# Results used later in three places of a four-layer network: leaky relu, pooled rows, a block's first channel sums

## The chip, the cores and the metric

The kernel runs on one core of a Trainium2 chip, in float32 throughout. The metric is the device time of one execution in microseconds (us); the time of a kernel is the median over its runs.

A core has five engines that each work off a list of instructions in order and wait for each other by semaphores: TensorE (PE, matmuls and transposes into PSUM; its weight loads are listed as PEld), VectorE (DVE), ScalarE (ACT), GpSimd (POOL) and SyncE (SP, which here issues the plain DMAs).[...]

## The reference

Four layers of 256 channels act on four images of 64 x 64 pixels; each normalises its input over groups of eight channels (`_gn`) and adds its result to it. Layer 0 is a deformable convolution with a feed-forward part, layer 1 a linear attention, layer 2 a 3 x 3 convolution with binarised weights, layer 3 a softmax attention in which keys and values come from the image pooled 2 x 2. Of these, the change touches the sampling and the feed-forward part of layer 0 and the pooling of layer 3:

```
        samp = _grid_sample(img, sg)
        mr = mask.reshape(n, H * W, G, P).transpose(0, 2, 1, 3).reshape(n * G, 1, H * W, P)
        dout = (samp * mr).sum(-1).reshape(n, G * GC, H * W).transpose(0, 2, 1).reshape(n, H, W, C)
        dout = jnp.einsum('nhwc,oc->nhwo', dout, outproj_w) + outproj_b
        x2 = _bn(inp + dout, bn2_g, bn2_b, bn2_m, bn2_v, 3)
...
        hmid = jax.nn.leaky_relu(jnp.einsum('nhwc,oc->nhwo', x3, fc1_w) + fc1_b, SLOPE)
        m = jnp.einsum('nhwc,oc->nhwo', hmid, fc2_w) + fc2_b
        return (inp + m).transpose(0, 3, 1, 2)
...
        theta = _conv1x1(x, theta_w, theta_b)
        xp = _maxpool2x2(x)
        phi = _conv1x1(xp, phi_w, phi_b)
        gi = _conv1x1(xp, g_w, g_b)
```

## The kernel before

Channels lie on the 128 partitions (two tiles of them, `KT` = 2); an image of 4096 pixels is worked on in eight blocks of 512 (`NB`). Each step is a Python generator that issues some instructions and yields a cost. `beside` (in `run`) steps one main generator and hands each of the others its share of the way by those costs. Under `ordered()` the order in which instructions are issued on PE, DVE, ACT and POOL is kept as written; SP's is not in that list.

The stages, in order: layer 0's first convolution for image 0; then `sample` for the images 0 to 3, each with other work beside it (convolutions of the other images beside image 0; from image 1 on, the feed-forward part of the image before in the first fifth, then its layer 1, and from image 2 on layers 2 and 3 of the image before that); then, without any gather left, the last image's feed-forward part, layer 1 and what remains of layers 2 and 3.

`sample` goes in rounds of 14 pixels, 293 per image; up to 16 rounds make a block of up to 224 pixels, 19 per image. In each round POOL issues four indirect DMAs (L592), which gather 128 rows each into a tile `g` (seven buffers). PE multiplies them with the weights `wm` (made by DVE, L583, four rounds at a time) and sums them into one half of the PSUM tile `acc` (L599). Two rounds make a unit, which fills that half. A unit that ends in round i is then passed on by work kept in `later`, at the head of the rounds that follow, ahead of their gathers:

- in round i + 1, `moved`: ACT copies the half to `at` (L604)
- in round i + 2, `turned`: PE transposes `at` into one half of the PSUM tile `dp` (L609)
- in round i + 3, `spread`: ACT copies that into the block's `dT`, twice (L624); `dT` has one buffer

After a block's last round i, `project` (PE, L632), `add` (DVE, L636) and `finish` (ACT, L641, with its sum read out, and a store by SP, L644) follow for the first channel tile in rounds i + 4, i + 5 and i + 6 and for the second one round later each. So `spread` of the next block's first unit stands in the same round as the second `project`, behind it. Entries of one round run in the order in which they were entered.

`feedforward` loads its weights, works out a gate per channel, folds it into `f1`, and goes through the eight blocks: for each of eight tiles of hidden channels a matmul into a PSUM bank (L717), then `leaky`: ACT writes slope times the value into `lk` (L173; two buffers), DVE takes the larger of that and the value into `hm` (L174). Then for each of two tiles 16 matmul instructions over `hm` (L724) and DVE's addition to the residual `xyf` (L725), DVE's statistics of the result (L110) and its store (L728). Each matmul of 512 columns is two instructions in the profile. The banks come from a rotation of three (`ps`), which the projections `po` and other work share.

`layer3` first goes through its eight blocks: load `x5` (L154), the theta matmul (L1074), ACT's copy with bias (L1075), DVE's two maxima for the pooling (`m1`, L1079, then `xq`, L1082), and then on `xq` the phi and g matmuls (L1087, L1089) and their copies (L1090 ACT, L1091 DVE). The attention over all pixels follows.

Of the kernel before, what the change touches and what calls it, by code (L numbers as in the profile page):

```python
# [9 lines left out]
F32 = mybir.dt.float32  # L10
I32 = mybir.dt.int32
AF = mybir.ActivationFunctionType
ALU = mybir.AluOpType
# [4 lines left out]
P = 128  # L18
N, C, H, W = 4, 256, 64, 64
HW = H * W  # L20
KT = C // P
NB = HW // 512
# [7 lines left out]
RP, WR, UR, BR = 14, 4, 2, 16  # L30
# [5 lines left out]
SLOPE = 0.01  # L36
# [35 lines left out]
class Net:  # L72
# [92 lines left out]
    def row(self, name):  # L165
        at, n = ROWS[name]
        return self.rows[:, at:at + n]

    def leaky(self, pool, out, ps, bias, low):

        nc = self.nc
        t = pool.tile([P, 512], F32, name="lk")
        nc.scalar.activation(t, ps, AF.Identity, bias=low, scale=SLOPE)  # L173
        nc.vector.scalar_tensor_tensor(out, ps, bias, t, ALU.add, ALU.max)  # L174

    def depthwise(self, acc, src, w, k, rows, cols, r0, bias=None, step=lambda cost: cost, out=None):

# [370 lines left out]
    def sample(self, n, ssum):  # L548
# [4 lines left out]
        nc, sp = self.nc, self.sp  # L553
# [34 lines left out]
        def gathered(sl, wm, acc, r):  # L588
            r4, acc = r % WR, acc[:, r % UR * P:(r % UR + 1) * P]
            g = self.gp.tile([P, G, 256], F32, name="g", bufs=7)  # L590
            for i in range(G):
                nc.gpsimd.indirect_dma_start(  # L592
                    out=g[:, i, :], out_offset=None, in_=table,
                    in_offset=bass.IndirectOffsetOnAxis(ap=sl.bitcast(I32)[:, r, i:i + 1], axis=0))


            for x in range(2):
                for i in range(G):
                    nc.tensor.matmul(acc[32 * i:32 * i + 32, :], wm[:, r4, 4 * i + 2 * x:4 * i + 2 * x + 2, :],  # L599
                                     g[:, i, x * P:(x + 1) * P], start=x == 0, stop=x == 1)  # L600
# [48 lines left out]
        for i, (b, r) in enumerate(order):  # L649
            for f in later.pop(i, ()):  # L650
                f()
            sl, rounds = blocks[b]
            if r % UR == 0:
                acc = next(accs)
            gathered(sl, wm, acc, r)
            if r == 0 and b + 1 < len(BLOCKS):
                load(b + 1)
            ends = r + 1 == len(rounds)
            if r % WR == 0:
                if r + WR < len(rounds):  # L660
                    nxt = weigh(b, r + WR)
                elif b + 1 < len(BLOCKS):
                    nxt = weigh(b + 1, 0)
            if r % UR == UR - 1 or ends:
                unit = rounds[r - r % UR:r + 1]
                todo = [partial(moved, acc, len(unit), i), partial(turned, len(unit), i), partial(spread, unit, b, i)]
                todo = list(enumerate(todo, i + 1))
                if ends:
                    todo += [(i + 4 + m + j, partial(f, b, m)) for m in range(KT) for j, f in enumerate((project, add, finish))]
                for j, f in todo:  # L670
                    later.setdefault(j, []).append(f)
            if r % WR == WR - 1 or ends:
                wm = nxt
            yield 1
# [5 lines left out]
    def feedforward(self, n, ssum, st):  # L680
        nc, tc, a = self.nc, self.tc, self.a
        with tc.tile_pool(name=f"fa{n}", bufs=1, side="right") as sp, \
                tc.tile_pool(name=f"fb{n}", bufs=2, side="right") as bp:
            f1 = sp.tile([P, KT, 4 * C], F32, name="f1")
            nc.sync.dma_start(f1, a["fc1_wT"])
            f2 = sp.tile([P, 4 * KT, C], F32, name="f2")
            nc.sync.dma_start(f2, a["fc2_wT"])
            sd = sp.tile([P, KT, 64], F32, name="sd")
            nc.sync.dma_start(sd, a["se_down_wT"])
            su = sp.tile([64, C], F32, name="su")  # L690
            nc.sync.dma_start(su, a["se_up_wT"])
            mean = sp.tile([P, KT], F32, name="mean")
            nc.vector.tensor_reduce(mean, ssum, AX.X, ALU.add)
            nc.vector.tensor_scalar(mean, mean, 1.0 / HW, None, ALU.mult)
            ps = self.ps()
            for k in range(KT):
                nc.tensor.matmul(ps[0:64, 0:1], sd[:, k], mean[:, k:k + 1], start=k == 0, stop=k == KT - 1)
            dn = sp.tile([64, 1], F32, name="dn")
            nc.scalar.activation(dn, ps[0:64, 0:1], AF.Relu, bias=self.vec("se_down_b")[0:64])
            yield 2  # L700
            ex = sp.tile([P, KT], F32, name="ex")
            for m in range(KT):
                ps = self.ps()
                nc.tensor.matmul(ps[:, 0:1], su[:, m * P:(m + 1) * P], dn, start=True, stop=True)
                nc.scalar.activation(ex[:, m:m + 1], ps[:, 0:1], AF.Sigmoid, bias=self.vec("se_up_b", m))

            for k in range(KT):
                nc.scalar.activation(f1[:, k], f1[:, k], AF.Identity, scale=ex[:, k:k + 1])  # L708
            yield 6
            for b in range(NB):  # L710
                x2 = self.block(bp, self.x2_d[n], b, "x2f")
                xy = self.block(bp, self.xy_d[n], b, "xyf")
                hm = bp.tile([P, 4 * KT, 512], F32, name="hm", bufs=1)
                for m in range(4 * KT):
                    ps = self.ps()
                    for k in range(KT):
                        nc.tensor.matmul(ps, f1[:, k, m * P:(m + 1) * P], x2[:, k], start=k == 0, stop=k == KT - 1)  # L717
                    self.leaky(bp, hm[:, m], ps, self.vec("fc1_b", m), self.low1[:, m:m + 1])
                    if m % 2:
                        yield 5  # L720
                for m in range(KT):
                    ps = self.ps()
                    for k in range(4 * KT):
                        nc.tensor.matmul(ps, f2[:, k, m * P:(m + 1) * P], hm[:, k], start=k == 0, stop=k == 4 * KT - 1)  # L724
                    nc.vector.tensor_tensor(xy[:, m], xy[:, m], ps, ALU.add)  # L725
                    yield 10
                self.stats(st, xy, b)
                nc.sync.dma_start(self.x3_d[n][:, :, b * 512:(b + 1) * 512], xy)  # L728


    def layer1(self, n, st, st2):
# [301 lines left out]
    def layer3(self, n, st, wide=False):  # L1033
        nc, tc, a = self.nc, self.tc, self.a
        M = HW // 4
        with tc.tile_pool(name=f"na{n}", bufs=1, side="left") as sp, \
# [17 lines left out]
            ps = self.ps()  # L1054
# [12 lines left out]
            th = sp.tile([P, HW], F32, name="th")  # L1067
            ph = sp.tile([P, M], F32, name="ph")
            gt = sp.tile([P, 8, P], F32, name="gt")
            for b in range(NB):  # L1070
                x = self.block(bp, self.x5_d[n], b, "x5", tag="pT")
                ps = self.ps()
                for k in range(KT):
                    nc.tensor.matmul(ps, tw[:, k], x[:, k], start=k == 0, stop=k == KT - 1)  # L1074
                nc.scalar.activation(th[:, b * 512:(b + 1) * 512], ps, AF.Identity, bias=tb)  # L1075

                m1 = bp.tile([P, KT, 256], F32, name="m1", tag="pe")
                v = x.rearrange("p k (x d) -> p k x d", d=2)
                nc.vector.tensor_tensor(m1, v[:, :, :, 0], v[:, :, :, 1], ALU.max)  # L1079
                v = m1.rearrange("p k (r d x) -> p k r d x", d=2, x=W // 2)  # L1080
                xq = bp.tile([P, KT, P], F32, name="xq", tag="m2")
                nc.vector.tensor_tensor(xq.rearrange("p k (r x) -> p k r x", x=W // 2),  # L1082
                                        v[:, :, :, 0], v[:, :, :, 1], ALU.max)
                yield 4
                ps = self.ps()
                for k in range(KT):
                    nc.tensor.matmul(ps[:, 0:P], fw[:, k], xq[:, k], start=k == 0, stop=k == KT - 1)  # L1087
                for k in range(KT):
                    nc.tensor.matmul(ps[:, P:2 * P], xq[:, k], gw[:, k], start=k == 0, stop=k == KT - 1)  # L1089
                nc.scalar.activation(ph[:, b * P:(b + 1) * P], ps[:, 0:P], AF.Identity, bias=fb)  # L1090
                nc.vector.tensor_tensor(gt[:, b], ps[:, P:2 * P], gb, ALU.add)  # L1091
                yield 2


            tv = th.rearrange("p (n j) -> p j n", j=NT)
            for b in range(NB):
                m2 = bp.tile([P, 512], F32, name="m2")
                for j in range(4):
# [27 lines left out]
                    ps = self.ps()  # L1126
# [4 lines left out]
                r = self.block(bp, self.x5_d[n], b, "r5", bufs=1)  # L1131
                for k in range(KT):
                    ps = self.ps()
# [169 lines left out]
```

## Time and profile before

| what | value |
|---|---|
| runs | 7858.98 us median (7857.48 to 7888.82, three runs) |
| profiled execution | 8957.1 us, mean granted TensorE clock 0.804 |
| image 0's gathers | 190 to 1983 us |
| image 1's gathers | 1983 to 3751 us |
| image 2's gathers | 3751 to 5589 us |
| image 3's gathers | 5592 to 7430 us |
| feed-forward parts | 2046 to 2389, 3809 to 4155, 5646 to 5994, 7480 to 7703 us |
| layer 3's pooling loops | 4620 to 4730, 6464 to 6572, 8011 to 8095, 8762 to 8787 us |

The profile is of one execution, which took longer than the runs without a profiler. A line of the groups reads: source line, engine, operation, output from inputs, shapes, count, then busy time and mean duration, then how long the engine stood idle just before these instructions and what ended most of that idle time. A releaser named "remote" or "issue" is one that the profile doesn't resolve. Ends of matmuls are modelled.

### The profile page before, as it was taken

How to read it: one execution, taken by the hardware profiler on the slowest of the kernel's cores; microseconds unless marked ns; L12 is line 12 of the kernel's file. 1: busy time of each engine (PE TensorE's matmuls, PEld its weight loads, DVE VectorE, ACT ScalarE, POOL GpSimd, SP SyncE). 2: the span in 40 equal slices, each digit the busy share in tenths (PEclk: the TensorE clock that was granted, in tenths of full speed). 3: DMA queues.
4: the chain of work that ended last, by engine and by line, in shares of the span. 5: the costliest groups of instructions: out<-in, count | busy, mean ns of one | idle time of the engine just before them, and what ended most of it. 6: DMA issues, size and time to landing. Idle time of an engine off the chain costs nothing. (4 is left out here: it accounts for less than half of the span.)

```text
span 8957.1 us, 94935 instructions
## 1 busy us (share of the span) xinstructions
PE 6029.8 (67%) x36020; PEld 3636.8 (41%) x36020; DVE 5176.0 (58%) x6393; ACT 2190.6 (24%) x4899; POOL 5162.6 (58%) x4950
## 2 busy tenths in 40 slices
PE   3354554447744447688776677887766778987899
PEld 2232332223422223244554443345544433664477
DVE  4344443443366667524777776227777772599734
ACT  1111111112211111122223222222232222455424
POOL 1666666566666666666666656666666561376410
PEclk7566675668866667799987787898878889998899
DMA  6455454445533334444443334444544333220131
GB/s 166 119 152 158 135 160 130 131 125 161 161 105 104 104 106 124 122 133 135 133 138 110 110 112 135 139 136 128 142 116 115 108 116 97 71 71 27 45 96 55
DMA packets 819976, 1059.01 MB, mean 118 GB/s; under 512 B 464320, under 2 KB 524864, under 8 KB 817984
## 3 DMA queue, kind: packets, MB, share of 16 engines
q0 software_dynamic: 225024, 614.77, 23.9%
q1 hardware_dynamic: 594496, 438.18, 17.1%
q8 instruction: 285, 4.67, 0.2%
q14 instruction: 171, 1.40, 0.0%
HBM read 883.86 MB, written 168.69 MB: 118 GB/s over the span
## 5 line engine op out<-in xcount | busy, mean ns | idle before, releaser
L592 POOL DMA_INDIRECT g<-tab,sl x4688 | 4628.4, 987 | 2800.6 <-issue 1224.9
L185 DVE SCALAR_TENSOR_TENSOR agg<-pad,vec,agg 128x1024 f32<-128x1024 f32 x2280 | 2934.3, 1287 | 61.7
L599 PE MATMUL acc<-g,wm 128*32 128x128 f32 x18752 | 1027.0, 336 | 2144.7 <-ACT at L604 1593.1
L599 PEld LDWEIGHTS acc<-g,wm 128*32 128x32 f32 x18752 | 564.6, 129 | 2620.9 <-ACT at L604 1791.9
L583 DVE TENSOR_TENSOR wm<-con,sl 128x1024 f32<-128x1024 f32 (+1 forms) x296 | 358.2, 1211 | 720.7 <-remote 575.2
L1018 PE MATMUL ps<-xd,w 128*128 128x256 f32 x3072 | 746.0, 395 | 31.5 <-issue 23.6
L624 ACT COPY dT<-dp 64x112 f32<-64x112 f32 x1176 | 286.9, 244 | 1543.1 <-remote 734.7
L1018 PEld LDWEIGHTS ps<-xd,w 128*128 128x128 f32 x3072 | 594.8, 199 | 150.7 <-issue 66.9
L717 PE MATMUL ps<-x2f,f 128*128 128x512 f32 x1024 | 503.1, 642 | 7.1 <-ACT f L708 4.0
L788 PE MATMUL ps<-xr,qw 128*128 128x512 f32 x768 | 474.4, 750 | 21.4 <-issue 8.2
L174 DVE SCALAR_TENSOR_TENSOR hm<-ps,vec,lk 128x512 f32<-128x512 f32 x256 | 190.7, 750 | 497.5 <-ACT lk L173 394.4
L724 PE MATMUL ps<-hm,f 128*128 128x512 f32 x1024 | 457.7, 601 | 0.1
L604 ACT COPY at<-acc 128x256 f32<-128x256 f32 (+1 forms) x588 | 218.5, 372 | 731.3 <-remote 670.3
L969 POOL TENSOR_TENSOR xd<-xp 128x640 f32<-128x640 f32 x64 | 79.5, 1270 | 507.0 <-ACT xp L981 412.7
L632 PE MATMUL po<-dT,ow 128*128 128x224 f32 (+1 forms) x1216 | 318.2, 414 | 51.5 <-DVE hm L174 15.6
L836 ACT COPY kt<-pt 128x512 f32<-128x512 f32 x256 | 149.7, 585 | 792.1 <-remote 350.7
L173 ACT ACTIVATE lk<-ps,low 128x512 f32<-128x512 f32 x256 | 174.1, 687 | 625.2 <-PE ps L717 479.1
L1128 PEld LDWEIGHTS ps<-gt,pT 128*128 128x128 f32 x2048 | 288.9, 222 | 70.7 <-issue 40.4
L1128 PE MATMUL ps<-gt,pT 128*128 128x128 f32 x2048 | 302.1, 309 | 17.3 <-ACT pT L1124 11.7
L201 POOL TENSOR_TENSOR ak<-ak,m 128x1024 f32<-128x1024 f32 x96 | 227.9, 2373 | 147.1 <-ACT m L200 143.6
L1108 PE MATMUL s<-ph,th 128*128 128x512 f32 x512 | 289.3, 674 | 26.8 <-ACT kt L836 10.0
L632 PEld LDWEIGHTS po<-dT,ow 128*128 128x128 f32 x1216 | 263.3, 231 | 105.7 <-issue 46.4
(243 smaller groups left out, 8071.3 us busy)
## 6 DMA issues: line engine op xcount, KB each, us to landing
g<-tab,sl POOLq DMA_INDIRECT x4688
x<-x SPq DMA_DIRECT2D x128, 512.0 KB
xr<-x SPq DMA_DIRECT2D x96, 512.0 KB
x<-in_x SPq DMA_DIRECT2D x64, 512.0 KB
tab<-xo SPq DMA_DIRECT2D x512, 64.0 KB
y<-yc SPq DMA_DIRECT2D x32, 512.0 KB
x2f<-x SPq DMA_DIRECT2D x32, 512.0 KB
xyf<-x SPq DMA_DIRECT2D x32, 512.0 KB
```

The source lines that it names most:

```text
L185: nc.vector.scalar_tensor_tensor(to, s, wt, acc, ALU.mult, ALU.add)
L583: nc.vector.tensor_tensor(wm[:, 0:nu], self.con("own").unsqueeze(1).unsqueeze(1).to_broadcast(sh), sl[:, r:r + nu, G:].unsqueeze(3).to_bro ...
L592: nc.gpsimd.indirect_dma_start(out=g[:, i, :], out_offset=None, in_=table, in_offset=bass.IndirectOffsetOnAxis(ap=sl.bitcast(I32)[:, r, i: ...
L599: nc.tensor.matmul(acc[32 * i:32 * i + 32, :], wm[:, r4, 4 * i + 2 * x:4 * i + 2 * x + 2, :], g[:, i, x * P:(x + 1) * P], start=x == 0, st ...
L624: nc.scalar.copy(dT[b][hs, :, q0:q0 + m * (v1 - v0)].rearrange("p g (v o) -> p g v o", o=m), dp[u][hs, v0:v1, :, s, 0:m].rearrange("p v g ...
L632: nc.tensor.matmul(po[m][:, 0:np_], self.ow[:, k, m * P:(m + 1) * P], dT[b][:, k, 0:np_], start=k == 0, stop=k == G - 1)
L717: nc.tensor.matmul(ps, f1[:, k, m * P:(m + 1) * P], x2[:, k], start=k == 0, stop=k == KT - 1)
L724: nc.tensor.matmul(ps, f2[:, k, m * P:(m + 1) * P], hm[:, k], start=k == 0, stop=k == 4 * KT - 1)
L788: nc.tensor.matmul(ps, qw[:, k, m * P:(m + 1) * P], x[:, k], start=k == 0, stop=k == KT - 1)
L1018: nc.tensor.matmul(ps[:, e], w[:, k, t, 2 * half + e, m * P:(m + 1) * P], v[:, 2 * half + e, k, t:t + 8], start=i % 6 == 0, stop=i % 6 == 5)
L1108: nc.tensor.matmul(s[i], tv[:, 4 * b + j], ph[:, i * 512:(i + 1) * 512], start=True, stop=True)
L1128: nc.tensor.matmul(ps[:, 0:P], pT[:, m], gt[:, m], start=m == 0, stop=m == 7)
```

## The change

Three edits, each of which issues an instruction later than before; the arithmetic and the number of compute instructions stay as they are.

1. In `feedforward`, the helper `leaky` is gone. ACT's part is issued with its matmuls as before; DVE's part is kept in a list of one (`waits`) and issued after ACT's part of the next tile. The residual's addition is kept the same way, and issued after the fourth `k` of the next tile's matmuls or after the next block's first ACT part; with the second tile's addition go the statistics and the store. The generator yields after every tile (2.5, before: 5 after every second) and after every four `k` of the second product (5, before: 10 after all eight). The costs' sum is the same.
2. In `layer3`'s first loop, a block is split into `first` (load, theta, the maxima) and `then` (phi, g and their copies); `then` of a block is issued after `first` of the next.
3. In `sample`, `spread` of a block's first unit is entered one round later, i + 4.

```
@@ -165,13 +165,6 @@
     def row(self, name):
         at, n = ROWS[name]
         return self.rows[:, at:at + n]
-
-    def leaky(self, pool, out, ps, bias, low):
-
-        nc = self.nc
-        t = pool.tile([P, 512], F32, name="lk")
-        nc.scalar.activation(t, ps, AF.Identity, bias=low, scale=SLOPE)
-        nc.vector.scalar_tensor_tensor(out, ps, bias, t, ALU.add, ALU.max)
 
     def depthwise(self, acc, src, w, k, rows, cols, r0, bias=None, step=lambda cost: cost, out=None):
 
@@ -664,7 +657,8 @@
             if r % UR == UR - 1 or ends:
                 unit = rounds[r - r % UR:r + 1]
                 todo = [partial(moved, acc, len(unit), i), partial(turned, len(unit), i), partial(spread, unit, b, i)]
-                todo = list(enumerate(todo, i + 1))
+
+                todo = [(i + 1 + j + (j == 2 and r < UR), f) for j, f in enumerate(todo)]
                 if ends:
                     todo += [(i + 4 + m + j, partial(f, b, m)) for m in range(KT) for j, f in enumerate((project, add, finish))]
                 for j, f in todo:
@@ -707,6 +701,22 @@
             for k in range(KT):
                 nc.scalar.activation(f1[:, k], f1[:, k], AF.Identity, scale=ex[:, k:k + 1])
             yield 6
+
+            waits = []
+
+            def leave():
+                if waits:
+                    waits.pop()()
+
+            def hidden(hm, m, ps, t):
+                nc.vector.scalar_tensor_tensor(hm[:, m], ps, self.vec("fc1_b", m), t, ALU.add, ALU.max)
+
+            def total(b, m, ps, xy):
+                nc.vector.tensor_tensor(xy[:, m], xy[:, m], ps, ALU.add)
+                if m == KT - 1:
+                    self.stats(st, xy, b)
+                    nc.sync.dma_start(self.x3_d[n][:, :, b * 512:(b + 1) * 512], xy)
+
             for b in range(NB):
                 x2 = self.block(bp, self.x2_d[n], b, "x2f")
                 xy = self.block(bp, self.xy_d[n], b, "xyf")
@@ -715,17 +725,21 @@
                     ps = self.ps()
                     for k in range(KT):
                         nc.tensor.matmul(ps, f1[:, k, m * P:(m + 1) * P], x2[:, k], start=k == 0, stop=k == KT - 1)
-                    self.leaky(bp, hm[:, m], ps, self.vec("fc1_b", m), self.low1[:, m:m + 1])
-                    if m % 2:
-                        yield 5
+                    t = bp.tile([P, 512], F32, name="lk")
+                    nc.scalar.activation(t, ps, AF.Identity, bias=self.low1[:, m:m + 1], scale=SLOPE)
+                    leave()
+                    waits.append(partial(hidden, hm, m, ps, t))
+                    yield 2.5
+                leave()
                 for m in range(KT):
                     ps = self.ps()
                     for k in range(4 * KT):
                         nc.tensor.matmul(ps, f2[:, k, m * P:(m + 1) * P], hm[:, k], start=k == 0, stop=k == 4 * KT - 1)
-                    nc.vector.tensor_tensor(xy[:, m], xy[:, m], ps, ALU.add)
-                    yield 10
-                self.stats(st, xy, b)
-                nc.sync.dma_start(self.x3_d[n][:, :, b * 512:(b + 1) * 512], xy)
+                        if k % 4 == 3:
+                            leave()
+                            yield 5
+                    waits.append(partial(total, b, m, ps, xy))
+            leave()
 
 
     def layer1(self, n, st, st2):
@@ -1067,7 +1081,7 @@
             th = sp.tile([P, HW], F32, name="th")
             ph = sp.tile([P, M], F32, name="ph")
             gt = sp.tile([P, 8, P], F32, name="gt")
-            for b in range(NB):
+            def first(b):
                 x = self.block(bp, self.x5_d[n], b, "x5", tag="pT")
                 ps = self.ps()
                 for k in range(KT):
@@ -1081,7 +1095,9 @@
                 xq = bp.tile([P, KT, P], F32, name="xq", tag="m2")
                 nc.vector.tensor_tensor(xq.rearrange("p k (r x) -> p k r x", x=W // 2),
                                         v[:, :, :, 0], v[:, :, :, 1], ALU.max)
-                yield 4
+                return xq
+
+            def then(b, xq):
                 ps = self.ps()
                 for k in range(KT):
                     nc.tensor.matmul(ps[:, 0:P], fw[:, k], xq[:, k], start=k == 0, stop=k == KT - 1)
@@ -1089,7 +1105,14 @@
                     nc.tensor.matmul(ps[:, P:2 * P], xq[:, k], gw[:, k], start=k == 0, stop=k == KT - 1)
                 nc.scalar.activation(ph[:, b * P:(b + 1) * P], ps[:, 0:P], AF.Identity, bias=fb)
                 nc.vector.tensor_tensor(gt[:, b], ps[:, P:2 * P], gb, ALU.add)
-                yield 2
+
+            xq = None
+            for b in range(NB + 1):
+                last, xq = xq, first(b) if b < NB else None
+                yield 3 if xq is not None else 0.5
+                if last is not None:
+                    then(b - 1, last)
+                    yield 3
 
 
             tv = th.rearrange("p (n j) -> p j n", j=NT)
```

## The prediction, made before the changed kernel ran

> **What bounds the kernel now.** I read the page first, then the busy times by stage, then what GpSimd (POOL) and TensorE (PE) wait for inside one image, and last the order of time around one block start. From the page, the busiest engine and the group that sets the pace:
>
> ```profile
> PE 6029.8 (67%) x36020; PEld 3636.8 (41%) x36020; DVE 5176.0 (58%) x6393; ACT 2190.6 (24%) x4899; POOL 5162.6 (58%) x4950
> ...
> L592 POOL DMA_INDIRECT g<-tab,sl x4688 | 4628.4, 987 | 2800.6 <-issue 1224.9 <-remote 592.8 <-PE acc L599 576.5
> ```
>
> No engine is full over the whole span, so the stages have to be taken apart. The busy times by stage (first and third image's gathers, then the gatherless tail):
>
> ```profile
> 190.00:1983.00 1793.00, 801.26 (x6260) 504.58 (x6261) 789.10 (x1041) 248.22 (x689) 1164.22 (x1172) 0.65 0.51 141
> ...
> 3751.00:5589.00 1838.00, 1371.53 (x8651) 818.03 (x8649) 1147.30 (x1367) 455.36 (x1105) 1152.58 (x1172) 0.85 0.44 127
> ...
> 7703.00:8757.00 1054.00, 893.28 (x3639) 622.63 (x3640) 784.40 (x1050) 495.91 (x740) 533.49 (x256) 0.92 0.21 64
> ```
>
> Columns: stretch, length, busy PE, PE weight loads, DVE, ACT, POOL, granted clock. A gather takes 0.95 us plus 0.30 us of issue, so a round of four cannot take less than 5.0 us and an image of 293 rounds not less than 1465 us. The four images take 1793, 1768, 1838 and 1838 us. What keeps POOL above its floor in the third image, by the instruction's own waits:
>
> ```profile
>   issue: 299.9, 979
>   PE acc L599: 201.0, 77
>   remote: 102.2, 54
> ```
>
> It waits 201 us for a g buffer that PE has not read yet. PE itself sits at the end of a loop with ACT: every second round its gather matmuls wait for the `at` copy. At a block start, in order of time:
>
> ```profile
> 4118.99 3.25 PE L632 MATMUL po<-dT,ow 128*128 128x224 f32 x8 [5.20 <-DVE hm L174]
> ...
> 4122.34 0.51 ACT L624 COPY dT<-dp 64x112 f32<-64x112 f32 x2 [3.60 <-PE po L632]
> 4122.85 0.37 ACT L604 COPY at<-acc 128x256 f32<-128x256 f32 x1
> 4123.28 0.64 PE L599 MATMUL acc<-g,wm 128*32 128x128 f32 x16 [1.03 <-ACT at L604]
> 4123.85 3.70 PE L717 MATMUL ps<-x2f,f 128*128 128x512 f32 x8
> ...
> 4127.39 0.38 PE L609 MATMUL dp<-ident,at 128*128 128x128 f32 x2
> ...
> 4128.18 0.56 ACT L641 ACTIVATE yb<-yb,bn_sh,bn_r 128x224 f32<-128x224 f32 x1
> ```
>
> The second projection releases the two dT copies, these hold up `at`, and PE stands for 1.03 us. So images 3 and 4 are paced by PE and ACT together, images 1 and 2 nearly by the gathers, the tail by DVE and PE.
>
> The profiled execution is 1098 us longer than the runs (8957 against 7859). Four gather floors (5860) plus the other stages (190+273+1054+200) give 7577, so the runs can hold at most some 280 us above the floor. The sums below are in us of the profiled span and are subtracted from 7859 unscaled.
>
> **What the Trainium skill says.** "PSUM — Partial Sum Buffer", section "PSUM bank collisions raise a hardware error", wants semaphores by bank and quadrant, not by address. The trace agrees: PE waits for the copy of one half of `acc` (1.03 us above) before it writes the other half. `dp` has two halves of a bank too, so the same must hold between a dT copy and the next transposes L609. The same page, section "Engine vs sequencer instructions", calls the ACT and DVE queues strict FIFO; dT, then at, then yb above go so. "SBUF — State Buffer", section "two separate sides", describes one port pair that DVE and GpSimd lock against each other; L1079 is 2.60 us beside POOL's L201 and 0.68 without.
>
> **Part 1, leaky relu and residual one step later.** Nothing is removed: 256 ACT L173, 256 DVE L174, 64 L725 stay, with the `stats` and the x3 store (SP) behind them. L174 idles 394 us for L173 in the trace. But DVE is busy only 1147 of 1838 us there, and those who wait for L174 at all add up to 18.1+15.6+11.2+5.4+1.8 = 52 us (PE's weight loads and matmuls counted twice). They wait for its end, and it still starts only when L173 ends: 0 gained, hidden by DVE's idle time. The x3 store is now emitted after the next block's x2f and xyf loads, on SP, which the hand order leaves out; PE waits for neither load in L717's list: 0. The lag could cost a PSUM bank (three, so a bank returns after three tiles): at most the 18+16 us that L632 already shows. I take 0. What stays is the finer grain: the 16 matmuls of L724 (7.1 us) split in two, so rounds without any feed matmul vanish. There PE stands 0.5 us for `at`; I find five such rounds in the third image's feed: 5 x 0.5 x 3 images = 7.5, of which I take **-6**; bounds -20 and +10.
>
> **Part 2, pooled rows one block later.** PE waits for xq 23.0 (matmuls) + 7.8 (loads) = 30.8 us. All of it lies in 8010 to 8096 us:
>
> ```profile
>   PE ps L1087: 23.0, 6
> ```
>
> and the busy times of that stretch:
>
> ```profile
> 8010.00:8096.00 86.00, 58.48 (x224) 37.05 (x224) 83.73 (x84) 48.98 (x70) 53.51 (x23) 0.84 0.17 55
> ```
>
> DVE is busy 83.73 of these 86 us with work that the change leaves as it is, so PE's wait is hidden behind DVE. In the final stretch (8757 to 8787) PE waits some 0.6 us per two blocks for the x5 load, whose issue may move a little ahead: 2 us. I take **-3**; bounds -30 (the whole wait counts) and +5 (x loads issued ahead of other loads on SP).
>
> **Part 3, a block's first spread a round later.** Removed: at each block start after the first the 1.03 us above, since dT no longer stands before `at`: 18 x 1.03 = 18.5 us of PE per image. Added: the next unit's transposes L609 in that later round now follow dT in the same bank, and dT stands in ACT's queue behind yb (L641, 0.56+0.19 us). Built, the changed program has 80 such waits of L609 on the dT copies, the old one 4. Behind the waiting L609 stand that round's gather matmuls and all of PE. In the example L609 starts at 4127.39 and yb ends at 4128.83; with dT's 0.51 and some 0.1 of hand-over PE would start at 4129.5: 2.1 us. Where ACT is ahead it is 0. Laid out so over 18 block starts in the third image: 0.6, 0.6, 2.1, 0, 0, 0, 0.4, 4.6, 10.2, 0, 2.0, 0.2, 2.1, 0, 2.0, 3.9, 2.0, 2.2. The three large ones are ACT's own lateness, which the `at` wait of the following round pays today, so I count them at 2.1: 22.5 us. Fourth image, same way: 21. Net +4.0 and +2.5 in the images that PE paces; in the other two, hidden by the gathers: **+6**. Bounds: -74 (four images, no new wait) and +77 (2.1 at all 72 starts).
>
> The sum is -6 - 3 + 6 = -3: 7856 us.
>
> **The rivals.** *A, no measurable change* (within 0.5% = 39 us, about what a measurement of this kernel tells from nothing): 7856, its own range 7830 to 7885. For it: every wait taken away has another right behind it. *B, faster*: ACT has yb done before PE comes to L609, as at six of 18 starts, and the runs without a profile are paced by PE in all images; then 74 + 6 + 10 = 90 less: 7769. Against it: 12 of 18 starts have a new wait, and the first image's PE is busy 801 of 1793 us. *C, slower*: the new wait of L609 on dT takes over. At 2.1 us everywhere it is 72 x (2.1 - 1.03) = 77 more: 7936. It decides from a mean new wait of 1.03 + 39/72 = 1.6 us on; I count 1.25. *D, part 1 does nothing* at all, DVE not being anyone's limit in the feed: 7862, inside A.
>
> **How the numbers follow.** A with D 0.54, B 0.28, C 0.18; B above C because a bank or an ACT slot freed early may help where my list cannot see. 7856 is A's. The range leaves out about half of B and half of C: 7790 to 7915. Faster, same, slower by 0.5%: 0.28, 0.54, 0.18.
>
> **What would show it.** Block starts after the change: no gap before L599 behind the second projection (part 3's gain), but a gap before L609 one round on, ended by the dT copies, of 0 to 2.1 us. L1087 no longer waiting for xq, with the stretch around it as long as before. L174's idle shorter, the feed stretches (346 us in the third image) shorter by at most some 5 us. I am wrong if the gathers' images shorten by over 10 us each, or if L609's new waits pass 1.6 us in the mean.

## The result, and the profile after

| | before | after |
|---|---|---|
| median of six runs, us | 7874.28 (7857.48 to 7888.82) | 7829.76 (7820.61 to 7842.59) |
| ratio | | 0.9947, interval 0.993 to 0.9965 |
| profiled execution, us | 8957.1; a second one 7879.1 | 7818.8 |

The changed kernel takes 0.53% less, 42 us (0.0053 x 7874), with a 95% interval of 28 to 55 us. That lies inside the predicted range of 7790 to 7915. It is also just past the 0.5% up to which the prediction spoke of no change, with an interval on both sides of that line. Its direction, 3 us less, was right; its size was not. The range took in about half of the rival B, and without that the result would lie at or past its lower end: the range of A alone ended at 7830.

The page of the changed kernel, the two lines that answer to those shown of before (line numbers shift with the edit: L592 of before is L585 here, and L599 is L592):

```profile
PE 6058.6 (77%) x36020; PEld 3582.1 (46%) x36020; DVE 5160.3 (66%) x6393; ACT 2188.9 (28%) x4899; POOL 5129.8 (66%) x4950
...
L585 POOL DMA_INDIRECT g<-tab,sl x4688 | 4595.9, 980 | 1724.0 <-issue 1308.3
```

POOL's idle time before the gathers is 1724 us where it was 2801, and no large part of it is "remote" any more. That is far more than 42 us, so the two profiles can't be set against each other as they are: the one of before was of an execution that took 1098 us longer than its runs. A second profile of the kernel before was therefore taken first (the first experiment below). Against it the busy times by stage, images 0 to 3, then the last feed-forward part and the tail up to the final pooled layer, first before (second profile):

```profile
186.00:1711.00 1525.00, 983.12 (x6342) 552.57 (x6342) 798.60 (x1059) 249.11 (x692) 1159.42 (x1172) 0.70 0.60 166
1711.00:3225.00 1514.00, 1128.23 (x6852) 565.89 (x6853) 1045.90 (x1043) 346.20 (x877) 1148.31 (x1172) 0.79 0.49 142
3225.00:4784.00 1559.00, 1271.34 (x8593) 773.94 (x8591) 1140.45 (x1365) 454.14 (x1102) 1151.55 (x1172) 0.91 0.51 150
4784.00:6356.00 1572.00, 1282.69 (x8653) 778.87 (x8651) 1141.67 (x1366) 456.20 (x1108) 1149.28 (x1173) 0.91 0.50 145
6356.00:6624.00 268.00, 248.90 (x667) 113.54 (x667) 73.86 (x108) 57.70 (x96) 0.64 (x1) 0.96 0.24 79
6624.00:7687.00 1063.00, 899.00 (x3657) 628.47 (x3657) 791.01 (x1066) 500.48 (x749) 533.75 (x256) 0.91 0.21 63
```

and after:

```profile
185.00:1705.00 1520.00, 998.81 (x6342) 556.88 (x6342) 799.84 (x1061) 250.05 (x692) 1154.60 (x1173) 0.68 0.60 167
1705.00:3220.00 1515.00, 1116.44 (x6851) 558.77 (x6852) 1044.95 (x1042) 345.67 (x877) 1150.58 (x1172) 0.81 0.49 142
3220.00:4761.00 1541.00, 1268.81 (x8598) 770.86 (x8596) 1139.35 (x1366) 453.14 (x1103) 1146.29 (x1173) 0.91 0.52 151
4761.00:6321.00 1560.00, 1283.09 (x8673) 779.05 (x8672) 1140.93 (x1369) 455.14 (x1108) 1144.19 (x1173) 0.91 0.51 146
6321.00:6583.00 262.00, 244.51 (x646) 111.40 (x645) 72.61 (x106) 56.74 (x94) 0.23 (x1) 0.96 0.24 79
6583.00:7629.00 1046.00, 886.07 (x3666) 618.93 (x3666) 786.64 (x1066) 500.69 (x751) 533.19 (x256) 0.92 0.21 65
```

The columns are those of the prediction; the last two are the DMA engines' share and GB/s. The two profiled executions are 60 us apart (7879 and 7819), more than the 42 us of the runs, so a stage's share is that of these two executions. Images 0 and 1 stand near the floor of 1465 us in both. Images 2 and 3 are 18 and 12 us shorter, the tail is 17 us shorter. The last feed-forward part is 6 us shorter in this cut, but it starts from where the last unit of gathers ends; from its own first to its last matmul it takes 222.7 us before and 221.7 after. So the gain is where layers 2 and 3 of an image stand beside other work, and not in the feed-forward parts.

POOL's own waits in front of its gathers in image 2, before (second profile) and after:

```profile
  issue: 323.1, 1060
  PE acc L599: 63.2, 42
```

```profile
  issue: 321.7, 1056
  PE acc L592: 48.4, 35
```

The wait for `acc`, 201 us in the profile that the prediction read, is 63 us in the second one.

### The profile page after: what moved, and what is told of

It is laid out like the page before. It is cut to its first block, busy times and chain, and to the rows that moved or that the text cites. A ratio compares the mean times of both kernels' runs of the same rounds, so it can differ in the third digit from the quotient of the medians.

```text
span 7818.8 us, 94940 instructions
## 1 busy us (share of the span) xinstructions
PE 6058.6 (77%) x36020; PEld 3582.1 (46%) x36020; DVE 5160.3 (66%) x6393; ACT 2188.9 (28%) x4899; POOL 5129.8 (66%) x4950
## 5 line engine op out<-in xcount | busy, mean ns | idle before, releaser
L585 POOL DMA_INDIRECT g<-tab,sl x4688 | 4595.9, 980 | 1724.0 <-issue 1308.3
L592 PE MATMUL acc<-g,wm 128*32 128x128 f32 x18752 | 1310.2, 320 | 1114.9 <-DMA g<-tab,sl 565.0
L592 PEld LDWEIGHTS acc<-g,wm 128*32 128x32 f32 x18752 | 642.7, 121 | 1824.3 <-DMA g<-tab,sl 806.3
L1032 PE MATMUL ps<-xd,w 128*128 128x256 f32 x3072 | 709.6, 383 | 8.4 <-DVE x L1012 4.2
L727 PE MATMUL ps<-x2f,f 128*128 128x512 f32 x1024 | 482.6, 619 | 4.3 <-ACT f L702 4.0
L802 PE MATMUL ps<-xr,qw 128*128 128x512 f32 x768 | 447.3, 713 | 22.9 <-issue 6.9
L602 PE MATMUL dp<-ident,at 128*128 128x128 f32 x1172 | 271.3, 319 | 72.1 <-ACT dT L617 71.8
L625 PE MATMUL po<-dT,ow 128*128 128x224 f32 (+1 forms) x1216 | 293.8, 392 | 21.2 <-DVE yb L629 8.3
L727 PEld LDWEIGHTS ps<-x2f,f 128*128 128x128 f32 x1024 | 192.3, 195 | 232.7 <-issue 220.8
L194 POOL TENSOR_TENSOR av<-av,m 128x1024 f32<-128x1024 f32 x96 | 226.9, 2363 | 102.2 <-ACT m L193 97.7
```

The source lines that it names most:

```text
L194: nc.gpsimd.tensor_tensor(acc, acc, m, ALU.add)
L585: nc.gpsimd.indirect_dma_start(out=g[:, i, :], out_offset=None, in_=table, in_offset=bass.IndirectOffsetOnAxis(ap=sl.bitcast(I32)[:, r, i: ...
L625: nc.tensor.matmul(po[m][:, 0:np_], self.ow[:, k, m * P:(m + 1) * P], dT[b][:, k, 0:np_], start=k == 0, stop=k == G - 1)
L802: nc.tensor.matmul(ps, qw[:, k, m * P:(m + 1) * P], x[:, k], start=k == 0, stop=k == KT - 1)
L1032: nc.tensor.matmul(ps[:, e], w[:, k, t, 2 * half + e, m * P:(m + 1) * P], v[:, 2 * half + e, k, t:t + 8], start=i % 6 == 0, stop=i % 6 == 5)
```

## The experiments

All ratios are to the kernel before, run side by side on the same chip; the interval is in brackets. The tail's times count from the end of the last gather. POOL's falling behind in an image is the start of a round's first gather, counted from the image's first gather, less 5.0 us for each round.

**The kernel before, a second time.** No edit.

> The kernel before, unchanged, for a second profile: the first profiled execution took 8957 us where the runs take 7859, the changed kernel's took 7819 where its runs take 7830. Theory S (the first profile caught one stretched execution): a span of 7840 to 7890 us, image gathers of 1520 to 1560 us each, PE waiting mostly for the gathers and not for `at`, a ratio to the kernel before of 1.000. Theory P (the kernel before reacts to the profiler, the changed one doesn't): again over 8700 us, with image gathers of 1770 to 1840 us.

Measured: ratio 0.9994 (0.9986 to 1.0003), profiled span 7879.1 us, images 1525, 1514, 1560 and 1572 us. Theory S holds: the first profile had caught one stretched execution. One of its marks is missing: most of the time that L599 stands idle still ends with an `at` copy, 639 us in the whole kernel where the first profile had 1593. What stretched it isn't known; its trace puts 593 us of POOL's idle time down to "remote", which the profile doesn't resolve. From here on this second profile stands for before.

**Part 1 alone.** Edit: part 1 of the diff above, nothing else.

> Part 1 alone (leaky relu's DVE half and the residual one step later, finer yields). The measured whole is about 42 us (0.53%, interval 0.35 to 0.70). Theory F (the feed-forward part carries it, since the three feed stretches beside gathers are the only ones that shorten): 30 to 45 us less, ratio 0.994 to 0.996, feed stretches 10 us shorter each. Theory of the prediction: 6 us less, ratio 0.999. Theory T (the first spread carries it): 0 to 6 us less here.

Measured: 0.9991 (0.9982 to 0.9999), some 7 us less. The prediction's 6 us fits in size, theory F falls: the three feed stretches beside gathers take 309.9, 305.8 and 307.9 us against 310.5, 307.8 and 308.3.

**Part 2 alone.** Edit: part 2 of the diff above, nothing else.

> Part 2 alone (pooled rows' matmuls a block later). Theory of the prediction: 3 us less, ratio 0.9996, the DVE being full in the only stretch in which PE waits. Theory Q (the whole wait of PE for the pooled rows counts): 20 to 30 us less, ratio 0.996 to 0.9975. Theories F and T: 0 to 3 us less.

Measured: 0.9963 (0.995 to 0.9977), 29 us less. Part 2 is nearly the whole gain, and the prediction's 3 us is wrong by a factor of ten. Theory Q gave the size; whether it gave the reason, the experiments that follow tell. The tail is 22 us shorter, image 2 15 us.

**Part 3 alone.** Edit: part 3 of the diff above, nothing else.

> Part 3 alone (a block's first spread one round later). Theory of the prediction: the new wait of the transposes on the dT copies outweighs the removed 1.03 us, 6 us more, ratio 1.001, between 0.9905 and 1.010. Theory T (the removed wait counts at the block starts of the images that PE paces or of all, and the new wait is hidden): 20 to 74 us less, ratio 0.991 to 0.9975. Theory F: within 0.1% of no change.

Measured: 0.9992 (0.9984 to 1.0), some 6 us less. PE's waits in image 2, before and with part 3 alone (waiting instruction, releaser, us in total, times, longest):

```profile
PE acc L599 <- ACT at L604: 170.5, 95, 9.3
```

```profile
PE acc L599 <- ACT at L604: 144.3, 76, 9.3
PE dp L609 <- ACT dT L624: 25.1, 12, 4.4
```

19 waits, 26 us, are gone, as many as the image has blocks; of the waits of 0.9 to 1.15 us, 5 are left of 22. So the wait at the block starts went, as said. A wait of L609 on dT has come in their place: 25.1 us, of which before had one of 5.4. The one pays for the other to within 7 us. The 6 us of the runs can't be placed: the two profiled executions are equally long (7879.5 us, and 7879.1 before). A block start shows it in the changed kernel, in order of time (lines between them left out):

```profile
4335.05 1.78 PE L625 MATMUL po<-dT,ow 128*128 128x224 f32 x8 [1.33 <-DVE yb L629]
...
4336.07 0.37 ACT L597 COPY at<-acc 128x256 f32<-128x256 f32 x1
4336.76 0.65 PE L592 MATMUL acc<-g,wm 128*32 128x128 f32 x16
...
4339.48 0.59 ACT L634 ACTIVATE yb<-yb,bn_sh,bn_r 128x224 f32<-128x224 f32 x1
...
4340.05 0.49 ACT L617 COPY dT<-dp 64x112 f32<-64x112 f32 x2
...
4340.60 0.44 PE L602 MATMUL dp<-ident,at 128*128 128x128 f32 x2 [1.68 <-ACT dT L617]
```

`at` is copied while the second projection still runs, and the gathers' matmuls follow that without a gap, where 1.03 us stood before. One round later the transposes wait 1.68 us, because dT stands behind yb on ACT.

**Part 2's yields alone.** The phi and g matmuls stay behind their own block's maxima:

```
-                yield 4
+                yield 3 if b < NB - 1 else 3.5
                 ps = self.ps()
...
-                yield 2
+                yield 3
```

> The kernel before with part 2's yields alone: 3 and 3 in place of 4 and 2 per block, 0.5 more once, the phi and g matmuls staying right behind their own block's maxima. What the other generators issue between layer 3's pieces moves; PE's wait for the pooled rows stays. Part 2 as a whole gave a ratio of 0.9963 (0.995 to 0.9977). Theory W (PE's wait for the pooled rows, with what follows it, costs the 28 us): no change, 0.999 to 1.001. Theory O (the gain is the order in which the rest of the tail falls, shifted by the yields): 0.995 to 0.998.

Measured: 0.9991 (0.9983 to 0.9999). Less than theory O asked for in the whole, but the tail is 14.8 us shorter with PE's wait for the pooled rows as it was (26.2 us against 26.5). All but some 2 us of that comes after the pooling.

**Pooled rows later, with the old yields.** Part 2 with this in place of its loop's yields:

```
+                if xq is not None:
+                    yield 4
+                if last is not None:
+                    then(b - 1, last)
+                    yield 2
```

> Part 2 with the old yields: the phi and g matmuls a block later, 4 behind a block's maxima and 2 behind its matmuls, no added 0.5, so that the rest of layer 3 keeps its place among the others. Theory W: the same gain as part 2, ratio 0.995 to 0.9977. Theory O: most of the gain gone, 0.9985 to 1.001.

Measured: 1.0024 (1.0016 to 1.0031), 19 us more. So using the pooled rows later, with nothing else changed, makes the kernel slower. PE's wait for xq in the tail's pooling fell from 26.5 to 9.1 us, and the tail didn't get shorter (1523.8 us against 1522.5). Theory W falls.

**PE's wait taken away, nothing moved.** The matmuls read loaded columns in place of the pooled rows:

```
-  nc.tensor.matmul(ps[:, 0:P], fw[:, k], xq[:, k], start=k == 0, stop=k == KT - 1)
+  nc.tensor.matmul(ps[:, 0:P], fw[:, k], x[:, k, 0:P], start=k == 0, stop=k == KT - 1)
...
-  nc.tensor.matmul(ps[:, P:2 * P], xq[:, k], gw[:, k], start=k == 0, stop=k == KT - 1)
+  nc.tensor.matmul(ps[:, P:2 * P], x[:, k, 0:P], gw[:, k], start=k == 0, stop=k == KT - 1)
```

> The kernel before, with the phi and g matmuls reading the first 128 columns of the loaded block x5 instead of the pooled rows xq (so the pooling's result is left out of keys and values; all instructions, their order and the yields stay). PE's wait for xq is gone, nothing is moved. Theory W: 20 to 30 us less, ratio 0.996 to 0.9975, the tail's pooling stretch about 10 us shorter. Theory O, and the prediction's step (PE's wait is hidden behind a full DVE): within 0.1% of no change, and the pooling stretch within 2 us of 75.6 us.

Measured: 0.9994 (0.9986 to 1.0003), no change that can be told. PE's wait in the tail's pooling, before (second profile):

```profile
PE ps L1087 <- DVE xq L1082: 26.5, 7, 6.2
```

It is gone altogether, and the tail is 11 us shorter, of which 7 stand in its first 400 us, before the pooling, and 4 after that. So the prediction was right that this wait is hidden, but for a few us. The pooling stretch is not quite as long as before (78.3 us from its first maximum to its last addition, against 83.5); why is in the next section.

**Parts 1 and 3 together.** Edit: the change without part 2.

> Parts 1 and 3 together, without part 2. Alone they gave 0.9991 (0.9982 to 0.9999) and 0.9992 (0.9984 to 1.0000). If they add up: 0.9983, some 13 us less. If both were noise: 0.9995 to 1.0005. If the prediction's sign for part 3 holds (6 us more): 1.0000.

Measured: 1.0004 (0.9996 to 1.0013). The two small gains don't add up; together nothing is left that can be told from no change. In this profile POOL falls behind by 46 us in the rounds 240 to 276 of image 2 where it is 39 us before, which takes away the 5 us that the image's first 60 rounds gained.

**Half a unit of cost, and nothing else.**

```
-                yield 2
+                yield 2 if b < NB - 1 else 2.5
```

> The kernel before with one number changed: the last block of layer 3's first loop yields 2.5 instead of 2, so that everything that follows in layer 3 is issued by half a unit of cost later among the others. No instruction of the pooling moves against another. The change's yields alone gave 0.9991 with the tail 14.8 us shorter, all of it after the pooling. Theory H (that half unit is what shortened the tail after the pooling): the tail 12 to 16 us shorter than 1522.5 us, ratio 0.998 to 0.9992. Theory D (3 and 3 in place of 4 and 2 did it): the tail within 3 us of before, ratio 0.9995 to 1.0005.

Measured: 0.9985 (0.9978 to 0.9992), 12 us less, the tail 18 us shorter (1504.2 us). Theory H holds: one cost that a loop reports, with no instruction of the pooling moved against another, gives 0.4 of part 2's gain (12 of 29 us), and most of what part 2 gives in the tail (18 of 22).

**Pooled rows later, old yields, half a unit more.** The last `then` of the kernel with the old yields yields 2.5.

> Pooled rows a block later, with 4 and 2 as before and the half unit more at the end. Without the half unit it was 1.0024. Theory H: the half unit gives back 15 us of the tail, ratio 1.0000 to 1.001, and what is missing to part 2's 0.9963 comes from 3 and 3 together with the deferral. Theory W2 (the deferral does its part once the half unit is there): 0.9955 to 0.998.

Measured: 0.9997 (0.9989 to 1.0005); tail 1505.1 us. The half unit gives 19 us of the tail back, as theory H has it; W2 falls.

**One unit more.** As the half unit, with 3.

> The kernel before with 1 more (3 instead of 2 in the last block of layer 3's first loop). If a later layer 3 is better in itself (its results wait less), the gain goes on: tail 15 to 30 us shorter, 0.996 to 0.9985. If it is a matter of which instruction stands before which at a few places, it can have either sign: 0.998 to 1.003.

Measured: 0.999 (0.9974 to 1.0005), which one run of 7928 us among 14 pulls up; the others took 7843 to 7860 us, and the median, 7848.8 against 7863.7, is 15 us less. The tail is 17 us shorter (1505.4 us), of which 11 after its first 400 us, against 17 with the half unit. The second half unit gives no more that can be told, and less in that part of the tail. Between the two theories this doesn't decide: both allow for it.

**An attempt at a better version.** The changed kernel with layers 2 and 3 spread out further:

```
-  beside(self.sample(n, ssum[n]), rounds, *behind(n - 1), (second(n - 2), SECOND, 0.2, 0.9))
+  beside(self.sample(n, ssum[n]), rounds, *behind(n - 1), (second(n - 2), SECOND, 0.2, 0.98))
```

> The changed kernel with layers 2 and 3 of the image before the last spread to 0.98 of the gathers' rounds instead of 0.9. In images 2 and 3 POOL falls behind its floor by some 30 to 42 us in the rounds 240 to 276, where the ends of layer 3 and of layer 1 meet. If crowding is what costs there: 10 to 30 us less than the changed kernel, ratio to the kernel before 0.991 to 0.9935. If the loss only moves to the last rounds: the changed kernel's 0.9947, within 0.001.

Measured: 1.001 (1.0002 to 1.0019), where the changed kernel has 0.9947: slower by 0.6%. In the rounds 240 to 276 POOL falls behind by 25 and 33 us in images 2 and 3 instead of 30 and 40, but in the rounds 120 to 240 by 23 and 22 instead of 12 and 10. The loss has moved and grown.

## Why the range held and the sum did not

The sum said 3 us less and 42 were measured. That the result lies in the range is luck: the range was stretched towards B, and the kernel did not get faster in B's way.

**The basis.** The prediction took the stretched profile's split ("images 3 and 4 are paced by PE and ACT together"; they are images 2 and 3 in the count used here) and subtracted its sum from 7859. The floor in it, 1465 us per image, was sound, and "at most some 280 us above the floor" was near: by the second profile it is 302. But in the second profile the images stand 49 to 107 us above the floor, not 303 to 373, and the median round takes 5.02 us in images 2 and 3 where the first profile had 6.0. So these images too are paced by the gathers in most of their rounds. The instruction that waits was the right one, the amount of waiting wasn't.

**Part 1**: -6 was said, -7 measured alone (interval 1 to 14). The reason given for the zeros, DVE's own slack, is borne out: no feed stretch is over 2 us shorter. The 6 us were to come from the finer grain in three of these stretches; they are 3.0 us shorter together, so the number fits, but at most half of it is found where it was put. That the finer grain makes these few us was not tested apart.

**Part 3**: +6 was said, -6 measured alone (interval 0 to 13). The mechanism is the predicted one in both halves, a wait gone at the block starts and a wait on dT at the next transposes, but the net went the other way. The sum had a slip: its eighteen waits, with the three large ones at 2.1, add up to 20.5 and not to 22.5, so 2 and not 4 us net for image 2. And both terms were off there: 18.5 removed were counted, 26.2 were removed; 19.7 were added (25.1 less 5.4).

**Part 2**: -3 was said, -29 measured alone. Here two steps failed.

The first is "DVE is busy 83.73 of these 86 us with work that the change leaves as it is". DVE is indeed full there, and the stretch is as long as its work. DVE's groups in that stretch, before (second profile):

```profile
L185 DVE SCALAR_TENSOR_TENSOR agg<-pad,vec,agg 128x1024 f32<-128x1024 f32 x39 | 50.2, 1286 | 0.9
L1082 DVE TENSOR_TENSOR xq<-m 128x256 f32<-128x256 f32 x8 | 13.5, 1690 | 0.3
L1079 DVE TENSOR_TENSOR m<-x 128x512 f32<-128x512 f32 x8 | 13.4, 1674 | 0.0
```

and with part 2 alone:

```profile
L185 DVE SCALAR_TENSOR_TENSOR agg<-pad,vec,agg 128x1024 f32<-128x1024 f32 x39 | 50.1, 1285 | 0.8
L1082 DVE TENSOR_TENSOR xq<-m 128x256 f32<-128x256 f32 x8 | 11.5, 1440 | 0.3
L1079 DVE TENSOR_TENSOR m<-x 128x512 f32<-128x512 f32 x8 | 8.9, 1118 | 0.0
```

The instructions are left as they are, their durations aren't: the same 16 maxima take 20.4 us instead of 26.9, and the stretch 74.6 us instead of 83.5. In all 13 profiles but the first the maxima take 20.4 to 27.2 us, and the stretch without them 54 to 57. Neither the yields alone (24.4 us) nor the later rows alone (27.2) bring the maxima down to 20.4; both together do. The pooling beside image 3's gathers, where POOL runs no L201, shows what they cost undisturbed:

```profile
L1079 DVE TENSOR_TENSOR m<-x 128x512 f32<-128x512 f32 x8 | 5.5, 682 | 0.0
...
L1082 DVE TENSOR_TENSOR xq<-m 128x256 f32<-128x256 f32 x8 | 3.4, 425 | 0.3
```

So 18 us of the 83.5 (26.9 less 8.9) are waits inside DVE's instructions. One pair in time, of DVE and of POOL, before (second profile):

```profile
6954.62 2.59 DVE L1079 TENSOR_TENSOR m<-x 128x512 f32<-128x512 f32 x1
6957.25 2.44 DVE L1082 TENSOR_TENSOR xq<-m 128x256 f32<-128x256 f32 x1
```

```profile
6954.32 5.10 POOL L201 TENSOR_TENSOR ak<-ak,m 128x1024 f32<-128x1024 f32 x2 [0.37 <-ACT m L200]
```

The two L201s end at 6956.67 and 6959.42, the maxima 0.55 and 0.28 us after them. All 12 maxima of this stretch that start while an L201 runs end so, 0.55 us after it (L1079) or 0.28 us (L1082). The Trainium skill, "SBUF — State Buffer", section "two separate sides", says that the port pair shared by DVE and GpSimd is an exclusive lock, which a DVE instruction needs if both its inputs lie in SBUF, and that whichever engine comes first "gets the pair for the whole instruction; the other fully blocks"; these ends agree with that. The prediction had both prices, 2.60 and 0.68 us, and put them to no use. The same is seen in the run in which PE's wait was taken away: there the maxima took 22.8 us, and the stretch was 5 us shorter. That the overlap with L201 is what differs between these runs is read from the traces; no run removed L201.

The second failed step isn't in the sum at all: part 2's changed yields have no term there, nor a reason why they should cost nothing. Part 2 makes their total 48.5 instead of 48, and by that half unit all that follows in layer 3 is issued later among layer 1's pieces. To see where it counts, the DVE instructions of two profiles were matched one by one, occurrence by occurrence, and the difference of their starts taken as a median over 40 us; us against before, less the offset that the two tails have 400 us after the last gather:

| kernel | 680 us in | 840 us | 1080 us | end |
|---|---|---|---|---|
| PE's wait taken away | -6 | -7 | -7 | -4 |
| later, old yields | -2 | 0 | 0 | +1 |
| later, old yields, half a unit | -2 | -10 | -18 | -16 |
| half a unit alone | -2 | -10 | -18 | -17 |
| one unit alone | -3 | -3 | -10 | -11 |
| yields alone (with the half unit) | -2 | -8 | -15 | -15 |
| part 2 | -9 | -15 | -22 | -21 |
| the whole change | -5 | -13 | -21 | -20 |

The kernels with the half unit, and only these, win 13 to 16 us between 680 and 1080 us (one unit wins 7); the pooling, some 580 to 665 us in, is a separate 5 to 9 us of part 2. What the half unit does there can be read at one place. PE, and the DVE instruction that needs L871's result, in order of time, before (second profile):

```profile
7269.94 3.27 PE L1134 MATMUL ps<-m,ww 128*128 128x512 f32 x4 [2.79 <-DVE m L1129]
7273.00 2.33 PE L1108 MATMUL s<-ph,th 128*128 128x512 f32 x4
7275.27 1.95 PE L871 MATMUL den<-pad,ld 128*64 128x512 f32 x4
...
7280.77 0.69 DVE L873 TENSOR_SCALAR rd<-den 128x512 f32<-128x512 f32 x1 [3.26 <-PE den L871]
```

and with the half unit alone:

```profile
7243.97 2.31 PE L871 MATMUL den<-pad,ld 128*64 128x512 f32 x4
...
7250.45 1.98 PE L1134 MATMUL ps<-m,ww 128*128 128x512 f32 x4
7250.56 0.69 DVE L873 TENSOR_SCALAR rd<-den 128x512 f32<-128x512 f32 x1
```

Before, layer 3's L1134 stands ahead on PE and waits 2.79 us for a DVE result that is queued behind several L185; layer 1's long L871 stands behind it. DVE then runs dry for 3.26 us until L871 is done. Half a unit later L871 goes first, PE works on it while DVE gets through its queue, and both of these waits are gone. Between 650 and 930 us after the last gather DVE has four idle gaps over 1.3 us before (2.84, 2.04, 3.72 and 3.26, together 11.9) and none with the half unit. The other profiles agree: in all six kernels without the half unit L1134 stands first and DVE has that gap of 3.26 us, its gaps together 8.3 to 11.9; in the kernels with it L871 stands first, and the gaps are 0 to 1.4. No run exchanged these two instructions and nothing else, so that the gain comes from such exchanges is read from the traces. DVE's waits over some 485 us of the tail behind the pooling, before and after the whole change (the xq of these lines is a tile of layer 1, not the pooled rows):

```profile
DVE xq L895 <- ACT pr L894: 35.4, 14, 6.3
...
DVE rd L873 <- PE den L871: 11.1, 3, 5.8
DVE den L1117 <- ACT pe L1115: 6.8, 5, 1.6
```

```profile
DVE xq L909 <- ACT pr L908: 33.8, 16, 4.6
...
DVE rd L887 <- PE den L885: 4.9, 2, 4.5
...
DVE den L1140 <- ACT pe L1138: 3.7, 3, 1.6
```

**What is left of part 2's 29 us.** The tail gives 22 and image 2 gives 15 in the profiled execution, which is 40 us shorter than that of before, against 29 in the runs; so the parts are known only to some 10 us. In image 2 it is the end: in the rounds 240 to 276 POOL falls behind its floor by 39 us before, by 28 with part 2 and by 30 with the whole change, but by 44 and 40 in the two kernels with the later rows and the old yields. In image 3 it is 41 us in both part 2 and before. Why the one image gains and the other doesn't stays open; PE's order at these rounds differs between the two images. Nor is it settled why later rows with the old yields cost 19 us, of which the profiles show 11, in the images.

**The rivals.** D, part 1 doing nothing at all, can't be told from what was measured. C's price, a mean new wait of 1.6 us at each start, wasn't reached: the trace with part 3 alone shows 77 us of PE's waits on dT in all four images, 1.07 us for each of 72 starts. B's reason, ACT being early enough, was not the one by which the kernel got faster. Of the two signs of being wrong that the prediction named, the first came true in half: images 2 and 3 shortened by over 10 us, images 0 and 1 didn't. Nor did the stretch around L1087 stay as long as before (76.8 us after the change, 83.5 before).

**The sum.** The parts alone give 7, 29 and 6 us, 42 together, which is what the whole gives. As parts 1 and 3 together give nothing, this agreement may be partly chance: in the rounds 240 to 276 of image 2 alone POOL falls behind by 28 to 46 us in the profiles of the kernels that share out layers 2 and 3 as before.

## What to carry to other kernels

Where generators are interleaved by costs, a changed yield is a change of the program behind it: cost it at every place that moves, or test it alone, before crediting the edit that it came with. On a full engine ask not only whether its work is kept, but also whether its instructions will meet the same neighbours, if their durations in the profile differ by a factor of two or more. And set the profiled span against the timed runs before reading shares: 8957 against 7859 us was a warning, and a second profile of the same kernel put the waits right.

## What the runs showed of the hardware that was not expected

In the second profile DVE's tensor_tensor L1079 on 128x512 took 0.63 to 2.59 us and the strided L1082 on 128x256 0.41 to 2.45 us, depending on POOL's tensor_tensor L201 beside them. Size is no protection: layer 3's L1117, which adds one number per partition, took 0.15 us (median), but 14 of them started while an L201 ran, and each of these ended 0.01 to 0.02 us after it. Below, the first of the two L201s ends at 7042.41:

```profile
7040.30 2.13 DVE L1117 TENSOR_TENSOR den<-den 128x1 f32<-128x1 f32 x1
```

```profile
7040.06 4.79 POOL L201 TENSOR_TENSOR av<-av,m 128x1024 f32<-128x1024 f32 x2 [2.70 <-ACT m L200]
```

The 14 took 17.3 us; less 0.15 us each, an estimated 15 us of DVE's time went there, beside the 18 us of the maxima. L1079, L1082 and L1117 read two tensors in SBUF. DVE instructions that read one of their two from PSUM weren't held up: L185, whose `agg` lies there, took at most 1.293 us, with or without an L201, and 240 of them started beside one; L1136, which adds a PSUM tile on 128x512, took at most 0.69 us, and ten did.
